# Layer 2's mixture of experts by lists: where the list is made, how deep the ring of gathered rows is, and when the output rows are fetched and summed

## The chip, the cores and the metric

The kernel runs on one core of one Trainium2 chip. The metric is the device time of one execution in microseconds. Three runs of the kernel before took 878.51, 871.72 and 876.23 us, median 876.23.

The core's engines work from queues of their own and wait for each other by semaphores: TensorE (PE in the profile; its weight loads are PEld), VectorE (DVE), ScalarE (ACT), GpSimd (POOL) and SyncE (SP), which issues most of the transfers.

## The reference

The input x is 8 sequences of 128 tokens of 128 numbers, f32. Four layers follow, each of an attention, a cross attention and a feed-forward part, and after each part `x = layernorm(x + part(x))`. The change lies in the feed-forward part of layer 2 and touches what stands next to it. That part is itself a small block: an attention, then eight experts of which each token uses two.

```python
        x = x + ao @ wo                                     # attention of the block
        h = _rmsnorm(x, ln2_w)
        probs = jax.nn.softmax(h @ router_w, axis=-1)
        topv, topi = jax.lax.top_k(probs, TOPK)             # 2 of 8
        topv = topv / jnp.sum(topv, axis=-1, keepdims=True)
        weights = jnp.sum(jax.nn.one_hot(topi, E) * topv[..., None], axis=-2)
        gate = jnp.einsum('bsd,edm->bsem', h, w_gate)       # d = 128, m = 448
        up = jnp.einsum('bsd,edm->bsem', h, w_up)
        act = jax.nn.silu(gate) * up * weights[..., None]
        moe = jnp.einsum('bsem,emd->bsd', act, w_down)
        return x + moe
```

After it come the layer norm and the first part of layer 3, a recurrence over the tokens of each sequence (a scan).

## The kernel before

The kernel doesn't compute all eight experts for every token. Class `ListedExperts` makes lists. The 1024 tokens are taken in two halves of 512. Each half has 1024 pairs of a token and one of its two experts; the pairs are sorted by expert and padded, each expert's to whole items of 128 rows, which gives at most 15 items a half (`N8`), 30 in all. The steps, by their methods:

- `rows` stores the half's normed tokens in DRAM. `route` makes the router's probabilities and ranks.
- `places(i)` counts, by products with ones (`ps_place` on PE) and small operations of DVE, which slot each pair has: its item `it` and its row `s` in it. From these come two sets of one-hot matrices, `s16` (tile `e_s`, on DVE) and `r16` (tile `e_r`, which holds the token's number in two digits: the partition, and j of 0 to 3). Before the change POOL makes `r16`: one operation for the first digit (L1004), six for the second (L1007) and two fills (L1009). `places` ends with each item's expert and with `place`, each pair's row in the output.
- `lists(i)` multiplies the two (`ps_ids`, PE), turns the digits into token numbers (`e_low` on ACT, `e_ids` on DVE), and issues 15 indirect gathers from the POOL queue (`e_xg`, L1030), one for each item's 128 rows of 512 bytes. All 30 share a ring of eight buffers, so that a gather waits for the transposition eight items earlier.
- `loaded(k)` has SP load item k's expert weights (704 KB) into one of five buffers; `turned(k)` transposes its rows (`ps_T` on PE, L1060; ACT copies them to `e_xT`, L1065); `up(k)` makes gate and up (`ps_g`, `ps_u` on PE; Silu to `e_g` on ACT, L1075; their product `e_h` on DVE, L1077); `down(k)` makes `ps_o` on PE, ACT copies it to `e_y` (L1087) and SP stores it to DRAM as `l_out` (L1088).
- `run` goes through the items k. Its order for PE is: transposition of k+1, gate and up of k, down of k-1, and then the extra steps given for k. The second half's `route`, `places` and `lists` are such steps, at k = 2, 6 and 8; the first half's sums are one at k = 17.
- `sums(i)` issues eight indirect gathers (`e_y`, L1114) that fetch each token's two output rows from DRAM, and adds them, weighted, to the block's x in eight DVE operations (`fin_h`, L1122). `f.norm` then makes the layer norm: statistics (L345, L346), a square root on ACT (`sd`, L335, which needs a table load), `rstd` (L337), four `x_nat` (L351). `f.turn` transposes the result (`ps_T`, L329; `x_T`, L409).

Around the items, `idle(n)` issues n products of 128x512 whose result isn't used; they keep PE busy. Layer 3's first part begins with a projection of each half (`ps_proj`), a gate and a product (`l_g`, ACT; `l_u`, DVE) and scans (`l_st`, DVE).

What sets the order: in this stage PE's instructions stand in the order of the source (`tc.manual_schedule` for PE). The other engines' orders are made by the scheduler when the kernel is built; their queues are then run strictly in that order. So a DVE operation that waits holds back all that stand behind it.

Of the kernel before, what the change touches and what calls it, by code (L numbers as in the profile page):

```python
# [10 lines left out]
BF16 = mybir.dt.bfloat16  # L11
# [4 lines left out]
ALU = mybir.AluOpType  # L16
# [4 lines left out]
P = 128  # L21
B = 8
T = 128
D = 128
# [117 lines left out]
N8 = (2 * 4 * T + E2 * (T - 1)) // T  # L142
# [16 lines left out]
def tile_decoder(  # L159
# [21 lines left out]
    nc = tc.nc  # L181
# [3 lines left out]
    work = ctx.enter_context(tc.tile_pool(name="work", bufs=3))  # L185
# [51 lines left out]
    def cst(name):  # L237
        a, b = CONST[name]
        return const_sb[:, a:b]
# [56 lines left out]
    def mm(dst, lhsT, rhs, start=True, stop=True):  # L296
        nc.tensor.matmul(dst, lhsT, rhs, start=start, stop=stop)  # L297
# [7 lines left out]
    def spread(ap, n):  # L305

        return ap.unsqueeze(2).to_broadcast([ap.shape[0], ap.shape[1], n])

    def repeat(ap, n):

        return ap.unsqueeze(1).to_broadcast([ap.shape[0], n, ap.shape[1]])

    def idle(n, rhs=None):

        ps = ps_sc.tile([P, 512], F32, tag="sc", name="ps_idle")
        for _ in range(n):
            mm(ps, begin_bf, repeat(begin_bf if rhs is None else rhs, 4))
# [597 lines left out]
    class ListedExperts:  # L915
# [52 lines left out]
        def places(self, i):  # L968

            used = self.used[i]  # L970
            ps = ps_out.tile([P, 5, 8], F32, tag="out", name="ps_place")
            for j in range(4):
                mm(ps[:, j], below_bf, used[:, j], True, j == 0)
                for k in range(j):
                    mm(ps[:, j], begin_bf, used[:, k], False, k == j - 1)
            for j in range(4):
                mm(ps[:, 4], begin_bf, used[:, j], j == 0, j == 3)
            tidx = cst("tidx")
            more = self.few("more", [P, 8, 4])
# [12 lines left out]
            nc.vector.tensor_reduce(slot, own.rearrange("p k j e -> p (k j) e"), AX.X, ALU.add)  # L992
            above = self.few("above", [P, 8, N8 - 1])
            nc.vector.scalar_tensor_tensor(
                above, repeat(tidx[:, 1:N8], 8), float(T), spread(slot, N8 - 1), ALU.mult, ALU.is_le
            )
            nc.vector.tensor_reduce(it, above, AX.X, ALU.add)
            nc.vector.scalar_tensor_tensor(s, it, -float(T), slot, ALU.mult, ALU.add)
            self.s16 = work.tile([P, 8, P], BF16, tag="g_gt", name="e_s16", bufs=1)
            nc.vector.tensor_tensor(self.s16, spread(s, P), repeat(tidx, 8), ALU.is_equal)  # L1000
            item = self.few("item", [P, 8, N8])
            nc.vector.tensor_tensor(item, spread(it, N8), repeat(tidx[:, 0:N8], 8), ALU.is_equal)
            self.r16 = self.few("r16", [P, 8, 2, N8], BF16)
            nc.gpsimd.tensor_scalar(self.r16[:, :, 0, :], item, cst("index"), None, ALU.mult)  # L1004
            for j in range(1, 4):
                for k in range(2):
                    nc.gpsimd.tensor_scalar(self.r16[:, 4 * k + j, 1, :], item[:, 4 * k + j, :], float(j), None, ALU.mult)  # L1007
            for k in range(2):
                nc.gpsimd.memset(self.r16[:, 4 * k, 1, :], 0.0)  # L1009
            past = self.few("past", [1, N8, 8])  # L1010
            nc.vector.tensor_tensor(past, spread(tidx[0:1, 0:N8], 8), repeat(ends[0:1], N8), ALU.is_ge)
            of = self.few("of", [1, N8])
            nc.vector.tensor_reduce(of, past, AX.X, ALU.add)
            self.experts[i] = self.few("exp", [1, N8], I32, 2)
            nc.vector.tensor_scalar_min(self.experts[i], of, 7.0)
            self.place[i] = self.few("place", [P, 8], U32, 2)
            nc.vector.tensor_copy(self.place[i], slot)

        def lists(self, i):

            ps = ps_out.tile([P, 2, N8], F32, tag="out", name="ps_ids")
            for k in range(8):
                mm(ps, self.s16[:, k, :], self.r16[:, k], k == 0, k == 7)
            self.ids[i] = self.few("ids", [P, N8], U32, 2)
            low = self.few("low", [P, N8])
            nc.scalar.copy(low, ps[:, 1])
            nc.vector.scalar_tensor_tensor(self.ids[i], ps[:, 0], 4.0, low, ALU.mult, ALU.add)
            for o in range(N8):
                self.xg[N8 * i + o] = xg = self.few("xg", [P, D], bufs=8)
                nc.gpsimd.indirect_dma_start(  # L1030
                    out=xg, out_offset=None, in_=self.rows_d[i],
                    in_offset=bass.IndirectOffsetOnAxis(ap=self.ids[i][:, o : o + 1], axis=0),
                )
# [53 lines left out]
            nc.scalar.copy(y, po)  # L1087
            nc.sync.dma_start(out=self.out_d[i][T * o : T * (o + 1), :], in_=y)  # L1088

        def run(self, pool, amid):  # L1090
            self.items = pool
            n = 2 * N8
            for k in range(4):
                self.loaded(k)
            self.turned(0)
            for k in range(n + 1):
                if k + 4 < n:
                    self.loaded(k + 4)
                if k + 1 < n:
                    self.turned(k + 1)  # L1100
                if k < n:
                    self.up(k)
                if k > 0:
                    self.down(k - 1)
                for step in amid.get(k, ()):
                    step()

        def sums(self, i, more):

            ys = []  # L1110
            for k in range(2):
                for j in range(4):
                    y = self.late(f"y{k}", [P, D], bufs=4)
                    nc.gpsimd.indirect_dma_start(  # L1114
                        out=y, out_offset=None, in_=self.out_d[i],
                        in_offset=bass.IndirectOffsetOnAxis(ap=self.place[i][:, 4 * k + j : 4 * k + j + 1], axis=0),
                    )
                    ys.append(y)
            h = work.tile([P, 4, D], F32, tag="fin_h", name="fin_h", bufs=2)
            for k in range(2):  # L1120
                for j in range(4):
                    nc.vector.scalar_tensor_tensor(  # L1122
                        h[:, j, :], ys[4 * k + j], self.w[i][:, k, j : j + 1], h[:, j, :] if k else more[:, j, :],
                        ALU.mult, ALU.add,
                    )
            return h
# [604 lines left out]
    def second_layers(f1, decay):  # L1731
        with tc.tile_pool(name="l2x", bufs=1, side="right") as keep:
# [3 lines left out]
            with tc.manual_schedule(engines={mybir.EngineType.PE}):  # L1736
# [38 lines left out]
                m = ListedExperts(w_moe2, msc("rw2"), 0.0, vec("ln2"), "l2")  # L1775
# [6 lines left out]
                f2 = Later()  # L1782
# [424 lines left out]
    f2 = second_layers(l1_ffn(x, xT), decay)  # L2207
# [174 lines left out]
```

## Time and profile before

| | us |
|---|---|
| runs, lowest, median, highest | 871.72, 876.23, 878.51 |
| the profiled execution's own time | 879.0 |
| its span | 877.2 |
| busy in it: PE, DVE, ACT, POOL | 727.6, 545.1, 418.1, 177.2 |
| first list: first ps_ids, first gather, first transposition | 582.61, 585.08, 588.13 |
| second list: first gather, thirteenth | 625.41, 650.20 |
| first half's output gathers, first and last issue | 651.44, 661.43 |
| last down product, its copy | 692.8 to 693.5, 693.60 |
| last half's output gathers done, last sum | 708.2 |

Times in the trace are counted from the span's start. A timeline row gives start, duration, engine, line, what is written from what, the number of instructions in the row and, in brackets, how long the engine stood idle before it and what released it; "issue" is idle time for which the profile shows no wait, "remote" a release by something that it can't name. A row of windows gives a stretch, then busy time of the engines in it, the clock granted to PE as a share of full speed, and the busy share of the DMA engines. A row of waits gives who waited for whom: total, number of times, longest. PE's ends are modelled by the profiler, and its records are pipelined, so neighbouring rows overlap a little.

### The profile page before, as it was taken

How to read it: one execution, taken by the hardware profiler on the slowest of the kernel's cores; microseconds unless marked ns; L12 is line 12 of the kernel's file. 1: busy time of each engine (PE TensorE's matmuls, PEld its weight loads, DVE VectorE, ACT ScalarE, POOL GpSimd, SP SyncE). 2: the span in 40 equal slices, each digit the busy share in tenths (PEclk: the TensorE clock that was granted, in tenths of full speed). 3: DMA queues.
4: the chain of work that ended last, by engine and by line, in shares of the span. 5: the costliest groups of instructions: out<-in, count | busy, mean ns of one | idle time of the engine just before them, and what ended most of it. 6: DMA issues, size and time to landing. Idle time of an engine off the chain costs nothing. (4 is left out here: it accounts for less than half of the span.)

```text
span 877.2 us, 14577 instructions
## 1 busy us (share of the span) xinstructions
PE 727.6 (83%) x4790; PEld 501.6 (57%) x4790; DVE 545.1 (62%) x1561; ACT 418.1 (48%) x963; POOL 177.2 (20%) x373
## 2 busy tenths in 40 slices
PE   8879999999988687439888879769997959888883
PEld 4758776665655454115345445449997726655552
DVE  4677786685476665898777766653424166656663
ACT  2234355333566663453186555625334422566662
POOL 1210100010011300001120203044442130056660
PEclk8689999999999799759999999987997978999997
DMA  9310000000000000000000000055896365011111
GB/s 358 121 37 1 1 1 1 1 0 1 1 1 1 1 1 1 1 0 1 0 1 1 1 1 1 13 190 142 263 328 198 97 277 217 1 34 37 33 35 40
DMA packets 22771, 53.57 MB, mean 61 GB/s; under 512 B 3904, under 2 KB 14144, under 8 KB 21280
## 3 DMA queue, kind: packets, MB, share of 16 engines
q1 hardware_dynamic: 20640, 47.55, 16.0%
q0 software_dynamic: 1472, 3.02, 1.5%
q10 hardware_dynamic: 576, 2.00, 0.6%
q8 instruction: 39, 0.64, 0.3%
q14 instruction: 44, 0.36, 0.1%
HBM read 46.39 MB, written 3.01 MB: 56 GB/s over the span
## 5 line engine op out<-in xcount | busy, mean ns | idle before, releaser
L534 DVE TENSOR_REDUCE at_mx<-ps_s 128x8 f32<-128x1024 f32 x48 | 56.9, 1216 | 42.2 <-PE ps_s L297 42.2
L537 ACT ACTIVATE at_s<-ps_s,at_mx 128x128 f32<-128x128 f32 x192 | 53.7, 390 | 38.1 <-DVE at_mx L534 38.1
L297 PEld LDWEIGHTS ps_o<-w_moe,e_h 128*128 128x128 f32 (+1 forms) x496 | 62.7, 198 | 12.6 <-issue 10.7
L297 PE MATMUL ps_o<-w_moe,e_h 128*128 128x128 f32 (+1 forms) x496 | 66.0, 283 | 4.7 <-issue 3.8
L546 ACT ACTIVATE at_pT<-ps_T 128x512 f32<-128x512 f32 x96 | 53.6, 601 | 33.4 <-PE ps_T L329 33.3
L297 PE MATMUL ps_idle<-begin_bf 128*128 128x512 bf16 x226 | 63.2, 419 | 4.0 <-DVE l_s L658 2.9
L329 PE MATMUL ps_T<-const_sb,at_s 128*128 128x128 f32 x384 | 60.5, 295 | 7.2 <-ACT at_s L537 5.1
L2119 POOL COPY l_wg<-w 128x64 f32 x192 | 49.2, 302 | 81.5 <-ACT l_wd L2115 53.3
L297 PEld LDWEIGHTS <-begin_bf 128*128 128x128 bf16 x273 | 28.0, 111 | 62.5 <-issue 41.2
L329 PEld LDWEIGHTS ps_T<-const_sb,at_s 128*128 128x128 f32 x384 | 46.2, 146 | 28.8 <-issue 10.7
L1077 DVE TENSOR_TENSOR e_h<-e_g,ps_u 112x512 f32<-112x512 f32 x30 | 20.6, 688 | 57.8 <-PE ps_u L297 32.2
L297 PEld LDWEIGHTS ps_acc<-l_wd,l_h 128*128 128x128 f32 x256 | 31.0, 191 | 38.4 <-ACT l_h L2141 38.4
L297 PE MATMUL ps_acc<-l_wd,l_h 128*128 128x128 f32 x256 | 37.1, 288 | 13.2 <-ACT l_h L2141 13.2
L805 ACT ACTIVATE x_p<-ps_s,x_mx 128x256 f32<-128x256 f32 x64 | 30.0, 474 | 33.9 <-DVE x_mx L801 26.3
L517 POOL TENSOR_TENSOR kx<-xa_k,const_sb 128x512 f32<-128x512 f32 x16 | 16.8, 1052 | 130.2 <-PE ps_s L297 74.1
L2115 ACT COPY l_wd<-w 64x128 f32 x96 | 28.4, 296 | 26.1 <-PE ps_acc L297 17.5
L297 PE MATMUL ps_s<-kvT,x_q 128*128 128x256 f32 x128 | 35.3, 402 | 4.0 <-ACT x_p L805 4.0
L297 PE MATMUL ps_av<-at_pT,vaug 128*32 128x128 f32 x768 | 31.1, 284 | 9.0 <-ACT at_pT L546 8.5
L335 ACT ACTIVATE sd<-ln_mv,eps 128x4 f32<-128x4 f32 x28 | 8.3, 297 | 62.7 <-DVE ln_mv L346 54.8
L894 DVE TENSOR_TENSOR e_h<-e_g,ps_u 128x512 f32<-128x512 f32 x32 | 21.8, 684 | 24.1 <-PE ps_u L297 20.8
L297 PE MATMUL ps_u<-e_xT,w_moe 128*112 128x128 f32 x240 | 34.4, 288 | 1.1 <-issue 1.1
L297 PE MATMUL ps_g<-e_xT,w_moe 128*112 128x128 f32 x240 | 34.5, 291 | 1.0 <-ACT e_xT L1065 1.0
(481 smaller groups left out, 1705.5 us busy)
## 6 DMA issues: line engine op xcount, KB each, us to landing
w_moe<-in_w_moe_dram SPq DMA_DIRECT2D x30, 704.0 KB
w<-in_w_moe_dram SPq DMA_DIRECT2D x10, 1024.0 KB
w_moe<-in_w_moe_dram SPq DMA_DIRECT2D x4, 768.0 KB
l_wd<-w SPq DMA_DIRECT2D x96, 32.0 KB
l_out<-e_y SPq DMA_DIRECT2D x30, 64.0 KB
sq_sb<-in_squares_dram SPq DMA_DIRECT2D x1, 1152.0 KB
row_sb<-in_rows_dram ACTq DMA_DIRECT2D x1, 784.0 KB
const_sb<-in_consts_dram ACTq DMA_DIRECT2D x1, 630.5 KB
```

Source lines behind the costliest of these rows:

```text
L297: nc.tensor.matmul(dst, lhsT, rhs, start=start, stop=stop)
L329: nc.tensor.transpose(ps[:, i, :], src[:, i, :], ident)
L335: nc.scalar.activation(sd, var, AF.Sqrt, bias=eps)
L517: nc.gpsimd.tensor_tensor(kx, repeat(job.k(b), 4), spread(cst(job.hm), T), ALU.mult)
L534: nc.vector.tensor_reduce(nmx[k], flat, AX.X, ALU.max, negate=True)
L537: nc.scalar.activation(sh[u][1][:, i // 4, i % 4, :], flat[:, i, :], AF.Identity, bias=nmx[1][:, i : i + 1])
L546: to_T(sh[u][g // 2][:, g % 2], lambda t: nc.scalar.activation(p, t, AF.Exp))
L805: nc.scalar.activation(pr[:, j, :], ps[:, j, :], AF.Exp, bias=mx[:, j : j + 1], accum_out=sm[:, j : j + 1])
L894: nc.vector.tensor_tensor(h[:, c, :], g, pu, ALU.mult)
L1077: nc.vector.tensor_tensor(self.h[k], g, pu[:C2], ALU.mult)
L2115: nc.scalar.copy(dst, src)
L2119: nc.gpsimd.tensor_copy(dst, src)
```

## The change

In five parts.

1. `r16` is made by two DVE operations, before `s16`, instead of by nine of POOL.
2. The second half's gathered rows have a ring of their own of 15 buffers (`e_xg1`); the first half's keep the ring of eight.
3. `run` becomes `step(k)`. The gathers of the output rows become a method of their own, `fetched(i)`, issued at k = 15 for the first half and after the loop for the second; the sums follow at k = 21 (before: both at k = 17). Both go through the four rows j of a token with its two experts inside; before, all first experts came before all second ones.
4. The second half's `places` and `lists` come one item earlier, at k = 5 and 7.
5. The idle products: 16 instead of 10 after the first list, 30 instead of 14 at the end, there ahead of the last sums. The first half's transpositions `f.turn(0)` move from the end to k = 29, between the last two down products.

```diff
-            self.s16 = work.tile([P, 8, P], BF16, tag="g_gt", name="e_s16", bufs=1)
-            nc.vector.tensor_tensor(self.s16, spread(s, P), repeat(tidx, 8), ALU.is_equal)
             item = self.few("item", [P, 8, N8])
             nc.vector.tensor_tensor(item, spread(it, N8), repeat(tidx[:, 0:N8], 8), ALU.is_equal)
             self.r16 = self.few("r16", [P, 8, 2, N8], BF16)
-            nc.gpsimd.tensor_scalar(self.r16[:, :, 0, :], item, cst("index"), None, ALU.mult)
-            for j in range(1, 4):
-                for k in range(2):
-                    nc.gpsimd.tensor_scalar(self.r16[:, 4 * k + j, 1, :], item[:, 4 * k + j, :], float(j), None, ALU.mult)
-            for k in range(2):
-                nc.gpsimd.memset(self.r16[:, 4 * k, 1, :], 0.0)
+            nc.vector.tensor_scalar(self.r16[:, :, 0, :], item, cst("index"), None, ALU.mult)
+            nc.vector.tensor_tensor(
+                self.r16[:, :, 1, :].rearrange("p (k j) o -> p k j o", j=4),
+                item.rearrange("p (k j) o -> p k j o", j=4),
+                tidx[:, 0:4].unsqueeze(1).unsqueeze(3).to_broadcast([P, 2, 4, N8]), ALU.mult,
+            )
+            self.s16 = work.tile([P, 8, P], BF16, tag="g_gt", name="e_s16", bufs=1)
+            nc.vector.tensor_tensor(self.s16, spread(s, P), repeat(tidx, 8), ALU.is_equal)
...
             for o in range(N8):
-                self.xg[N8 * i + o] = xg = self.few("xg", [P, D], bufs=8)
+                self.xg[N8 * i + o] = xg = (self.late if i else self.few)(
+                    f"xg{i}", [P, D], bufs=N8 if i else 8
+                )
...
+        def fetched(self, i):
+
+            self.ys = {}
+            for j in range(4):
+                for k in range(2):
+                    self.ys[k, j] = y = self.late(f"y{k}", [P, D], bufs=4)
                     nc.gpsimd.indirect_dma_start(
                         out=y, out_offset=None, in_=self.out_d[i],
                         in_offset=bass.IndirectOffsetOnAxis(ap=self.place[i][:, 4 * k + j : 4 * k + j + 1], axis=0),
                     )
-                    ys.append(y)
+
+        def sums(self, i, more):
+
             h = work.tile([P, 4, D], F32, tag="fin_h", name="fin_h", bufs=2)
-            for k in range(2):
-                for j in range(4):
+            for j in range(4):
+                for k in range(2):
                     nc.vector.scalar_tensor_tensor(
-                        h[:, j, :], ys[4 * k + j], self.w[i][:, k, j : j + 1], h[:, j, :] if k else more[:, j, :],
+                        h[:, j, :], self.ys[k, j], self.w[i][:, k, j : j + 1], h[:, j, :] if k else more[:, j, :],
                         ALU.mult, ALU.add,
                     )
             return h
...
                 m.lists(0)
-                idle(10)
+                idle(16)
+            pe = mybir.EngineType.PE
+            with tc.manual_schedule(engines={pe}):
                 m.weights_of(0)
                 f = Finish(None)
                 with tc.tile_pool(name="l2m", bufs=1) as pool:
-                    m.run(pool, {
+                    m.items = pool
+                    amid = {
                         1: (lambda: f2.done(1, last, 1),),
                         2: (lambda: m.route(1, f2.h2T),),
-                        6: (lambda: m.places(1),),
-                        8: (lambda: m.lists(1),),
+                        5: (lambda: m.places(1),),
+                        7: (lambda: m.lists(1),),
                         9: (lambda: m.weights_of(1),),
-                        N8 + 2: (lambda: f.norm(0, m.sums(0, f2.xx[:, 0:4, :])),),
-                    })
+                        N8: (lambda: m.fetched(0),),
+                        N8 + 6: (lambda: f.norm(0, m.sums(0, f2.xx[:, 0:4, :])),),
+                        2 * N8 - 1: (lambda: f.turn(0),),
+                    }
+                    for k in range(2 * N8 + 1):
+                        m.step(k)
+                        for step in amid.get(k, ()):
+                            step()
+                    m.fetched(1)
+                    idle(30)
                     f.norm(1, m.sums(1, f2.xx[:, 4:8, :]))
                 epool.__exit__(None, None, None)
-                idle(14)
-                f.turn(0)
             return f
```

`step(k)` holds what the loop of `run` held for item k, in the same order.

More of the change, by code (lines that the diff above doesn't have):

```diff
@@ L1088, in down, with step @@
             nc.sync.dma_start(out=self.out_d[i][T * o : T * (o + 1), :], in_=y)
-        def run(self, pool, amid):
-            self.items = pool
+        def step(self, k):
             n = 2 * N8
[L1093 to L1110, printed above, removed]
-            for k in range(2):
-                for j in range(4):
-                    y = self.late(f"y{k}", [P, D], bufs=4)
+            if k == 0:
+                for o in range(4):
+                    self.loaded(o)
+                self.turned(0)
+            if k + 4 < n:
+                self.loaded(k + 4)
+            if k + 1 < n:
+                self.turned(k + 1)
+            if k < n:
+                self.up(k)
+            if 0 < k <= n:
+                self.down(k - 1)
+        def fetched(self, i):
[3 more added lines that the diff above has]
+                    self.ys[k, j] = y = self.late(f"y{k}", [P, D], bufs=4)
                     nc.gpsimd.indirect_dma_start(
@@ L1117, in sums @@
                     )
-                    ys.append(y)
+        def sums(self, i, more):
             h = work.tile([P, 4, D], F32, tag="fin_h", name="fin_h", bufs=2)
-            for k in range(2):
-                for j in range(4):
+            for j in range(4):
+                for k in range(2):
                     nc.vector.scalar_tensor_tensor(
-                        h[:, j, :], ys[4 * k + j], self.w[i][:, k, j : j + 1], h[:, j, :] if k else more[:, j, :],
+                        h[:, j, :], self.ys[k, j], self.w[i][:, k, j : j + 1], h[:, j, :] if k else more[:, j, :],
                         ALU.mult, ALU.add,
```

## The prediction

> **What bounds the kernel now.** I first read the table of windows through the expert stage, to see where TensorE stops being busy.
>
> ```profile
> 620.00:630.00 10.00, 9.72 (x93) 9.50 (x92) 4.17 (x10) 3.65 (x10) 6.52 (x11) 1.00 0.87 249
> 630.00:640.00 10.00, 10.00 (x91) 9.77 (x90) 2.75 (x4) 3.88 (x12) 4.72 (x6) 1.00 0.90 265
> 640.00:650.00 10.00, 10.00 (x94) 10.00 (x93) 2.75 (x4) 3.98 (x11) 2.95 (x4) 1.00 1.00 380
> 650.00:660.00 10.00, 7.41 (x66) 7.04 (x64) 2.03 (x5) 2.12 (x6) 7.54 (x8) 1.00 0.76 244
> 660.00:670.00 10.00, 7.39 (x32) 6.91 (x33) 5.33 (x19) 4.86 (x9) 3.34 (x4) 0.51 0.49 121
> ```
>
> The columns are PE, PEld, DVE, ACT and POOL busy, then granted clock, DMA share and GB/s. From 630 to 650 PE is full: the stage is bound by it, at 2.75 us an item (ps_o of items 16 and 17 start at 648.76 and 651.51). From 650 to 670 it is neither full nor, later, at full clock. The timelines of PE, DVE, ACT and POOL there say why.
>
> ```profile
> 654.26 1.06 PE L297 MATMUL ps_o<-w_moe,e_h 112*128 112x128 f32 x8
> 660.98 2.08 PE L297 MATMUL ps_o<-w_moe,e_h 112*128 112x128 f32 x8 [3.34 <-issue]
> 668.61 1.90 PE L297 MATMUL ps_o<-w_moe,e_h 112*128 112x128 f32 x8
> 672.20 1.06 PE L297 MATMUL ps_o<-w_moe,e_h 112*128 112x128 f32 x8
> ```
> ```profile
> 651.78 0.69 DVE L1077 TENSOR_TENSOR e_h<-e_g,ps_u 112x512 f32<-112x512 f32 x1 [2.06 <-PE ps_g L297]
> 654.55 0.35 DVE L1122 SCALAR_TENSOR_TENSOR fin_h<-e_y,e_w,l_xx 128x128 f32<-128x128 f32 x1 [2.09 <-DMA e_y<-l_out,e_place]
> 658.87 0.65 DVE L1122 SCALAR_TENSOR_TENSOR fin_h<-e_y,e_w,l_xx 128x128 f32<-128x128 f32 x2 [0.75 <-issue]
> 660.24 0.69 DVE L1077 TENSOR_TENSOR e_h<-e_g,ps_u 112x512 f32<-112x512 f32 x1 [0.72 <-remote]
> ```
> ```profile
> 655.90 0.60 ACT L1075 ACTIVATE e_g<-ps_g 112x512 f32<-112x512 f32 x1 [2.39 <-PE ps_T L1060]
> 664.47 0.27 ACT L1087 COPY e_y<-ps_o 128x128 f32<-128x128 f32 x1 [7.97 <-PE ps_T L1060]
> ```
> ```profile
> 651.44 0.94 POOL L1114 DMA_INDIRECT e_y<-l_out,e_place  x1 [0.30 <-issue]
> ```
>
> The down products of items 18, 19, 20 and 21 start at 654.26, 660.98, 668.61 and 672.20: 17.94 us for three items that take 8.25, a loss of 9.7 us. Two things hold them up.
>
> First, the sums. Four sums of the first half stand in DVE's queue ahead of item 19's e_h; the gathers that feed them start at 651.44, and the fourth sum ends at 659.52.
>
> Second, less plain: e_h of item 19 runs not at 659.52 but at 660.24, and ACT copies item 18's ps_o at 664.47, although PE's record has that product finished at 655.32 (654.26 + 1.06). What waits for PE is released up to 9.1 us late. The same shows under an earlier row of gathers, issued 1.25 us apart from 625.41 to 630.47:
>
> ```profile
> 628.34 1.04 PE L297 MATMUL ps_u<-e_xT,w_moe 128*112 128x128 f32 x8
> 629.21 1.06 PE L297 MATMUL ps_o<-w_moe,e_h 112*128 112x128 f32 x8
> ```
> ```profile
> 631.17 0.69 DVE L1077 TENSOR_TENSOR e_h<-e_g,ps_u 112x512 f32<-112x512 f32 x1 [3.75 <-PE ps_T L1060]
> ```
> ```profile
> 632.58 0.27 ACT L1087 COPY e_y<-ps_o 128x128 f32<-128x128 f32 x1 [3.03 <-PE ps_u L297]
> ```
>
> There ps_u ends at 629.38 and is used at 631.17 (1.8 us late), and ps_o ends at 630.27 and is used at 632.58 (2.3 late). A third place is the stage's start, under gathers in close order from 585 to 599: ps_u of item 1 ends at 596.60 and its e_h runs at 600.89. From 634.5 to 650 the gathers stand 2.75 us apart, because the ring of eight makes each wait for a transposition, and nothing is late (ps_o ends 649.82, its copy starts 649.85). So **late release goes with gathers in close order**. That it is caused by them is my inference.
>
> **The change, part by part** (differences in us; minus is faster).
>
> *Sums and output gathers.* The DVE order of the built kernel does not put the sums six items later: five of them still stand between e_h of items 18 and 19, three between 19 and 20. What changes is the supply. The second half's input gathers are out of the way, so the first output gather waits only for the landing of item 14's store (issued 644.77, landing marks about 648.1) and can start at 648.4, not 651.44; the eighth is issued at 657.1, not 661.43. The fifth is issued at 653.4 and lands 2.2 to 4.2 later (the range of 656.43 to 658.62 and of 652.69 to 656.87), so item 19's e_h, due at 654.5 (651.78 + 2.75), is free of sums at 656.5 to 658, half covered by the 2.06 us that DVE idles per item. Close gathers end 4.3 us earlier, hence also the late releases. Bounds: 0 (as late as now) and -9.7. I take **-4.5**, near the 4.3. On ACT the sd and its table load (1.28 + 0.30) now come ahead of item 19's e_y; both stood ahead of item 22's e_xT before, so nothing further waits.
>
> *Ring of fifteen.* It removes this wait of POOL:
>
> ```profile
> POOL e_xg L1030 <- PE ps_T L1060: 19.4, 9, 3.7
> ```
>
> That wait cost PE nothing, since PE was full. What goes with it is the spacing: fifteen gathers now run at 1.25 us from 623.4 to about 642, beside full PE and a DMA share of 0.87 to 1.00. Ten more than now are in close order. Lower row: the five at 625 to 631 cost PE 0.30 (ps_T of three items at 630.10, 632.90, 635.90: 5.80 for 5.50), 0.06 each, so +0.6. Upper row: the ten from 650 to 662 stand beside a loss of 9.7, 0.97 each, so +9.7. By the end of the five the lateness was 2.3, already over DVE's 2.06 of slack; ten more gathers span 4.5 items, and 0.24 to 2.2 beyond slack in each (2.3 to the start's 4.3) is 1 to 10. I take **+3.5**. A rule speaks against this term: the Trainium skill, "SBUF — State Buffer" (opening part on the two sides), holds that transfers and engines use separate ports and cannot slow each other; by it the term would be 0 and the total 3.5 lower. The late releases at 631 and 664 do not fit that rule, though no run here yet isolates them.
>
> *List on DVE.* Two e_r operations go ahead of at_o (579.69), which leads through at_oT, ps_o and ps_ids to the first gather. Nearest row: e_item, 128x120, 0.28 at 578.37, issued 0.19 apart. Two cost 0.4 to 0.6: **+0.4**. POOL's e_r ended at 581.62, before ps_ids (582.61), so nothing is won there. In the second list PE's 0.27 wait for POOL's e_r (at 624.32) goes: **-0.3**; DVE has slack for the rest. The step one item earlier only moves work.
>
> *Sixteen idle products for ten.* Ten took 3.37 (582.87 to 586.24), then PE stood 1.89 until the first ps_T at 588.13. Six more take 2.0, so 0.1 late, or 2.6 at half clock (0.43 each), 0.7 late. If the clock (0.74 in 590 to 600) stays up for one more stretch, the 3.82 of ps_g and ps_u at 590.49 becomes 2.1; but item 0's e_g waits for ACT's table load until 593.93 anyway. Bounds -3.4 and +0.7; I take **-0.7**.
>
> *End of the stage.* Four transpositions (0.60 at 696.38) now precede the last down product: +0.6. The thirty idle products take 6.84 (14 took 3.19) and end about 701; ps_proj (1.93) then ends at 703, before the last sum at 708.21, so they are hidden. In DVE's queue l_u (0.65, at 706.07 between gathers before) moves behind the aggregates with the scans (1.39) and still ahead of rstd: +0.65; the new order of sums leaves fewer statistics behind the last one: about -0.05 to -0.5. I take **+1.2** in all, bounds +0.5 and +2.
>
> *Sum*: -4.5 + 3.5 + 0.4 - 0.3 - 0.7 + 1.2 = -0.4. The profiled execution took 879.0 (span 877.2), so it would take 878.6; on the median of the runs, 876.2 (871.7 to 878.5), 875.8, say **876**.
>
> A second rule may be set beside the gathers' landing: "DMA: Bandwidth & Descriptors", section on the anatomy of a SWDGE transfer, gives 2.0 us plus bytes/436e3, an estimated 2.15 for 64 KB; by it alone the fifth gather would land at 655.6 and the sums would hold nothing. The 4.2 measured at 652.69 under load says it can be twice that.
>
> **Rivals.**
>
> *Close gathers cost as much everywhere as at 650 to 662* (slower). Place: items 13 to 18 under the fifteen, then 18 to 20 under the eight. Price: +9.7 for ten more, and only -1.9 at the sums (two gathers fewer at 0.97), with the rest +0.6: +8.4, 884.6; a half-clock stretch of 3.4 us more makes 888. It decides once e_h or e_y follow PE's end by more than some 3 us for several items. For it: 4.3 and 9.1 us late at two of three places. Against: 0.30 lost at the third, which is the place in question.
>
> *Late release goes with the sums, not the gathers* (faster). Then the fifteen cost 0, the stall shrinks by 8.7, the start gives 2: -8.7 + 0.4 - 0.3 - 2 + 1.2 = -9.4, 866.8. For it: 650 to 670 is the only place with a large loss, and the sums are there. Against: ACT's copy at 664.47 waits for no sum.
>
> *The change does not do what it says.* DVE still meets the sums at item 19; if the output gathers land as late as now, -1 + 0.6 + 0.6 = +0.2, 876.4.
>
> **How the numbers follow.** Forecast 0.40, slower rival 0.28, faster rival 0.18, no effect 0.14. What differs by under 1% (8.8 us) can hardly be told from no change here. Faster 0.18, same 0.54, slower 0.28. The range reaches from below the faster rival, 865, to the slower one at half clock, 889.
>
> **What would show it.** Right: POOL's fifteen gathers 1.25 us apart, then DVE's e_h 3 to 4 us after PE's ps_u in several of items 11 to 17, ps_T more than 2.75 apart there; output gathers starting some 3 us sooner after item 14's store; items 18 to 21 in about 13 us, not 17.9. Wrong: PE busy 10.00 in every window under the fifteen gathers (ring term 0), items 18 to 21 again in 18 us, or ps_proj after the last sum.

## The result, and the profile after

The changed kernel takes 888.73 us (median of six runs, 887.42 to 892.05); the kernel before 876.84 (871.72 to 878.67, six runs). The medians lie 11.9 us apart, 1.4%. The record's ratio of the runs, which is not the ratio of the medians, is 1.0169, with an interval of 1.0146 to 1.0193. By either the change makes the kernel slower. The profiled execution took 890.67 with a span of 888.8, against 879.0 and 877.2 before, so its span is 11.6 us longer.

First the table of windows of the changed kernel, through the same part of the expert stage and with the same columns as before (PE, PEld, DVE, ACT and POOL busy, granted clock, DMA share, GB/s).

```profile
620.00:630.00 10.00, 8.72 (x78) 8.28 (x76) 1.66 (x4) 2.34 (x7) 7.14 (x8) 1.00 0.82 229
630.00:640.00 10.00, 4.46 (x14) 3.44 (x15) 0.00 (x0) 1.13 (x3) 7.01 (x8) 0.55 0.47 129
640.00:650.00 10.00, 7.99 (x44) 7.50 (x44) 2.06 (x3) 2.73 (x8) 0.00 (x0) 0.59 0.59 165
650.00:660.00 10.00, 10.00 (x94) 10.00 (x93) 2.59 (x4) 3.99 (x10) 0.00 (x0) 1.00 0.90 272
660.00:670.00 10.00, 9.99 (x91) 9.79 (x89) 2.87 (x8) 2.80 (x8) 5.73 (x6) 1.00 0.90 289
670.00:680.00 10.00, 5.83 (x36) 5.80 (x37) 5.06 (x18) 5.35 (x10) 3.14 (x3) 0.83 0.63 193
```

The loss is in one place. In 630 to 640, where PE was full before, it now runs 14 products in ten microseconds instead of 91, and DVE runs nothing at all. POOL's 7.01 are the second half's gathers: the fifteen stand 1.25 us apart from 620.73 to 638.20. From 650 to 660, with no gather on POOL, PE is full again. The next hole, 670 to 680, follows the eight output gathers (662.57 to 671.38).

PE's timeline in the first hole:

```profile
628.62 1.16 PE L297 MATMUL ps_o<-w_moe,e_h 112*128 112x128 f32 x8 [1.17 <-issue]
...
631.25 2.05 PE L297 MATMUL ps_g<-e_xT,w_moe 128*112 128x128 f32 x8 [1.36 <-issue]
633.46 0.37 PE L297 MATMUL ps_u<-e_xT,w_moe 128*112 128x128 f32 x1 [0.16 <-issue]
634.86 0.37 PE L297 MATMUL ps_u<-e_xT,w_moe 128*112 128x128 f32 x1 [1.03 <-issue]
636.26 0.37 PE L297 MATMUL ps_u<-e_xT,w_moe 128*112 128x128 f32 x1 [1.02 <-issue]
...
642.76 2.08 PE L297 MATMUL ps_o<-w_moe,e_h 112*128 112x128 f32 x8 [0.53 <-DVE e_h L1079]
...
648.20 1.06 PE L297 MATMUL ps_o<-w_moe,e_h 112*128 112x128 f32 x8
```

Eight products of one ps_u, which take 1.04 us in an undisturbed item, are strung out over nine, and the idle time before them is "issue": they wait for nothing that the profile shows. The down products of items 9, 10 and 11 start at 628.62, 642.76 and 648.20, 19.58 us for two items that take 5.50. ACT and DVE, in their timelines:

```profile
639.09 0.60 ACT L1077 ACTIVATE e_g<-ps_g 112x512 f32<-112x512 f32 x1 [7.90 <-remote]
```
```profile
642.01 0.69 DVE L1079 TENSOR_TENSOR e_h<-e_g,ps_u 112x512 f32<-112x512 f32 x1 [13.45 <-remote]
```

The table of waits from 620 to 645 puts it in sums (who waited for whom: total, times, longest):

```profile
DVE e_h L1079 <- remote: 13.5, 1, 13.5
...
ACT e_g L1077 <- remote: 7.9, 1, 7.9
PEld ps_u L297 <- issue: 6.5, 6, 1.6
PE ps_u L297 <- issue: 5.8, 8, 1.0
```

None of these names a transfer or another engine's work; the table's other rows of ACT and DVE name PE. ACT's e_g needs ps_g, whose last product ends at 633.30 by PE's record; it runs at 639.09, 5.8 us late. This is the late release of the prediction, now as a whole item's stall. It ends about 4 us after the last close gather is issued (638.20 to 642.0).

The other places that the prediction named. The output gathers start at

```profile
662.57 0.94 POOL L1113 DMA_INDIRECT e_y<-l_out,e_place  x1 [23.43 <-DMA l_out<-e_y]
```

held by item 14's store, as worked out: 6.1 us after the start of that item's down product, where it was 8.2 before and 5.1 had been worked out. The end of the stage, in DVE's timeline:

```profile
718.07 0.35 DVE L1123 SCALAR_TENSOR_TENSOR fin_h<-e_y,e_w,fin_h 128x128 f32<-128x128 f32 x1 [0.86 <-DMA e_y<-l_out,e_place]
...
718.88 0.66 DVE L1860 TENSOR_TENSOR l_u<-l_g,ps_proj 64x512 f32<-64x512 f32 x1
719.58 1.36 DVE L1862 TENSOR_TENSOR_SCAN l_st<-l_A,l_u 64x128 f32<-64x128 f32 x4
720.87 0.14 DVE L337 RECIPROCAL rstd<-sd 128x4 f32<-128x4 f32 x1
721.04 1.12 DVE L351 TENSOR_SCALAR x_nat<-fin_h,ln_mv,rstd 128x128 f32<-128x128 f32 x4
```

Here l_u does stand behind the last sum, and ps_proj (done at 712.55) doesn't hold it. The same points in both traces give the account (start of the down product ps_o of an item):

| from, to | before | after | difference |
|---|---|---|---|
| span's start to e_rank, the stage's first list | 574.03 | 572.26 | -1.8 |
| e_rank to ps_o of item 0 | 22.40 | 22.24 | -0.2 |
| items 0 to 8 | 30.03 | 30.04 | 0.0 |
| items 8 to 12 | 11.29 | 26.41 | +15.1 |
| items 12 to 18 | 16.51 | 16.50 | 0.0 |
| items 18 to 21 | 17.94 | 14.58 | -3.4 |
| items 21 to 28 | 19.15 | 19.15 | 0.0 |
| item 28 to x_nat | 19.37 | 19.86 | +0.5 |
| x_nat to the span's end | 166.5 | 167.8 | +1.3 |

Before rounding they add to 11.6. Against 2.75 us an item, items 9 to 11 lose 15.4 us here; the expectations below count 14.4. The first row lies ahead of the change. In the last, the second half's ps_proj takes 3.27 instead of 2.49, +0.8.

### The profile page after: what moved, and what is told of

Read it like the earlier page. It is cut to its first block, busy times and chain, and to the rows that moved or that the text cites. A ratio compares the mean times of both kernels' runs of the same rounds, so it can differ in the third digit from the quotient of the medians.

```text
span 888.8 us, 14604 instructions
## 1 busy us (share of the span) xinstructions
PE 734.5 (83%) x4812; PEld 504.0 (57%) x4812; DVE 546.5 (61%) x1565; ACT 417.8 (47%) x963; POOL 172.3 (19%) x355
## 5 line engine op out<-in xcount | busy, mean ns | idle before, releaser
L297 PE MATMUL ps_idle<-begin_bf 128*128 128x512 bf16 x248 | 67.0, 412 | 3.2 <-DVE l_s L658 2.1
L297 PEld LDWEIGHTS <-begin_bf 128*128 128x128 bf16 x295 | 29.9, 109 | 64.5 <-issue 41.0
L297 PE MATMUL ps_u<-e_xT,w_moe 128*112 128x128 f32 x240 | 37.0, 293 | 8.0 <-issue 7.9
L297 PEld LDWEIGHTS ps_u<-e_xT,w_moe 128*112 128x112 f32 x240 | 32.6, 195 | 9.2 <-issue 9.2
```

## The experiments

r_after and r_after2 are the changed kernel unaltered. The runs came on four chips, each group with the kernel before on the same one. The ratios are the record's, to that kernel (they differ a little from those of the medians); the kernel before took 868.86 us on chip A, 876.63 on B, 874.42 on C and 875.52 on D. "At 2.75" means that the down products of the items stand 2.75 us apart, which is PE full.

| kernel, chip | us | ratio, interval | down product to down product |
|---|---|---|---|
| e1_shared8, A | 870.27 | 1.0013, 0.9991 to 1.0036 | 9 to 18 at 2.75; 19, 20: 7.25, 4.52 |
| e2_ring15_only, A | 875.99 | 1.0076, 1.0050 to 1.0102 | 13: 6.68; 19, 20: 8.94, 4.74 |
| e3_paced15, A | 869.57 | 1.0006, 0.9988 to 1.0025 | 9 to 18 at 2.75; 19, 20: 7.84, 4.50 |
| e4_paced_all, A | 865.04 | 0.9955, 0.9938 to 0.9973 | 9 to 27 at 2.75 |
| r_after, B | 892.41 | 1.0168, 1.0114 to 1.0222 | 9, 10, 11: 5.61, 13.51, 4.86; 19, 20: 7.47, 4.50 |
| e5_no_weights, B | 892.37 | 1.0168, 1.0123 to 1.0212 | 10, 11: 15.61, 5.32; 18, 19, 20: 7.76, 5.49, 3.12 |
| e6_plain_rows, B | 876.12 | 0.9986, 0.9966 to 1.0006 | 9 to 18 at 2.75; 19, 20: 7.43, 5.49 |
| e7_late_sums, B | 894.29 | 1.0197, 1.0147 to 1.0248 | 9, 10, 11: 5.60, 13.61, 4.82; 19, 20: 7.46, 4.49 |
| r_after2, C | 890.17 | 1.0191, 1.0145 to 1.0237 | 9, 10, 11: 4.14, 14.71, 4.62; 19, 20: 7.40, 4.35 |
| e2b_ring15_only, C | 888.58 | 1.0169, 1.0124 to 1.0215 | 11, 12: 15.49, 5.49; 19, 20: 7.27, 4.51 |
| e3b_paced15, C | 877.09 | 1.0023, 0.9999 to 1.0047 | 9 to 18 at 2.75; 19, 20, 21: 6.35, 7.91, 3.73 |
| e8_best, C | 868.02 | 0.9931, 0.9901 to 0.9961 | 11 to 21 at 2.75; 22, 23: 5.31, 4.52 |
| e9_best2, D | 866.48 | 0.9897, 0.9873 to 0.9921 | 9, 10, 13: 4.35, 3.08, 3.22; 15 to 27 at 2.75 |
| e10_in_order, D | 889.42 | 1.0149, 1.0114 to 1.0184 | 9, 10, 11: 4.17, 14.62, 5.13; 19, 20: 7.66, 4.48 |
| e11_threes, D | 876.48 | 1.0018, 0.9997 to 1.0039 | 9 to 17 at 2.75; 18, 19, 20: 4.55, 9.12, 3.89 |
| e12_two_an_item, D | 878.45 | 1.0035, 1.0010 to 1.0061 | 13, 14: 2.92, 3.79; 18, 19, 20: 4.34, 8.90, 5.46 |

### Which part of the change: the ring

e1 is the changed kernel with the ring of eight for both halves; e2 and e2b are the kernel before with the ring of fifteen as its only change. The edit of e1 (e2's is the reverse of it, in the kernel before):

```diff
-                self.xg[N8 * i + o] = xg = (self.late if i else self.few)(
-                    f"xg{i}", [P, D], bufs=N8 if i else 8
-                )
+                self.xg[N8 * i + o] = xg = self.few("xg", [P, D], bufs=8)
```

> The changed kernel with one part undone: the second half's gathered rows share the ring of eight again. Theory A (close gathers): fifteen gathers 1.25 us apart slow PE itself. Then at most some five run in close order, the 14.4 us lost between the down products of items 8 and 11 fall below 1, and the time falls from 888.7 to 873 to 877. Rival B (another part of the change, such as the list made on DVE or the second list one item earlier, causes the stall): 886 to 890 as now.

> The kernel before with one part of the change alone: a ring of fifteen of its own for the second half's gathered rows. Theory A: the stall of some 14 us appears here too, 886 to 892 against 876.8 before. Rival B: 875 to 878, as before.

On chip A the ring alone costs 7.1 us, and without it the rest of the change is worth nothing that can be measured (+1.4, its interval holding 1). But chip A shows the cost in another form. In e2's timeline of PE:

```profile
633.82 1.93 PE L297 MATMUL ps_g<-e_xT,w_moe 128*112 128x128 f32 x8 [2.09 <-DMA w_moe<-in_w_moe_dram]
```

PE waits for an expert's weights, item 13 comes 3.9 us late, and no release is late under the close gathers. Where the rest of the 7.1 us lies isn't shown, since the kernel before has no trace on chip A. Items 1 and 2 of this chip's kernels come 3.2 and 3.6 us after their forerunners, where they come 5.2 and 6.7 in the profile before. So A couldn't test the mechanism, and the same kernel was run again on C beside the unaltered change.

> The changed kernel, unaltered, to stand beside the next three on one chip. Two kinds of chip have shown so far: on one (kernel before 876 to 877) the changed kernel takes 888 to 892 and PE is released late under close gathers; on the other (kernel before 868.9) nothing was late behind PE. Where the kernel before takes 876 here, 888 to 893; where it takes 869, theory A gives no PE stall and 871 to 876 by late weights alone.

> The kernel before with the ring of fifteen alone, a second time, to stand beside the changed kernel on one chip. Where the kernel before takes 876: theory A gives a stall of 12 to 15 us under the fifteen gathers, 887 to 892, which would put the whole loss down to this one part. Where it takes 869: 875 to 877, as the first time. If on a chip of the first kind it stays under 880, the loss needs another part of the change as well.

There the ring alone costs 14.2 us (888.58 - 874.42), all but 1.6 of the change's 15.8. The row of windows of e2b is that of the changed kernel, and so is PE's timeline, single products of ps_u 0.7 to 2.1 us apart:

```profile
630.00:640.00 10.00, 3.47 (x15) 2.77 (x16) 0.00 (x0) 1.13 (x3) 7.56 (x9) 0.63 0.49 134
```

### What about the ring: the close order, or the depth

e3 and e3b keep the ring of fifteen and all else of the change, but each of the second half's gathers is put one item later than the one before, by a copy of POOL that needs the item's e_y.

```diff
+            if after is not None:
+                nc.gpsimd.tensor_copy(xg[:, 0:1], after[:, 0:1])
             nc.gpsimd.indirect_dma_start(
...
+                    for o in range(N8):
+                        amid[7 + o] = amid.get(7 + o, ()) + (lambda o=o: m.gathered(1, o, m.last_y),)
```

> The changed kernel with its ring of fifteen, but the second half's gathers issued one an item: ahead of each, POOL copies one column of the item's e_y into the gather's buffer, so it waits for that item. Theory A: with 2.75 us between gathers the 14.4 us at items 9 to 11 are gone though the ring is fifteen, 873 to 877. Rival C (the ring's place or size in memory causes the stall, not the spacing): 886 to 890. The eight output gathers still come in close order, so the 6.3 us lost at items 19 and 20 stay in both.

> The changed kernel with its ring of fifteen and the second half's gathers paced one an item, a second time. Where the kernel before takes 876: theory A gives items 9 to 18 at 2.75 us and 874 to 878; a ring of fifteen that stalls whatever the spacing gives 888 or more. Where it takes 869: 869 to 871 as the first time.

On C the loss under the input rows is gone, and the row of windows is full:

```profile
630.00:640.00 10.00, 10.00 (x94) 10.00 (x93) 2.75 (x4) 3.95 (x10) 4.45 (x7) 1.00 0.99 309
```

Same ring, same gathers, same other changes: what costs is that they come close. What is left of the change against before is then +2.7 (interval -0.1 to +4.1). Two finer doses on D say how close is too close: e11 issues them in groups of three, a group every third item, and e12 two an item.

```diff
-                        amid[7 + o] = amid.get(7 + o, ()) + (lambda o=o: m.gathered(1, o, m.last_y),)
+                        amid[7 + o // 3 * 3] = amid.get(7 + o // 3 * 3, ()) + (lambda o=o: m.gathered(1, o, m.last_y),)
```

(e12: `7 + o // 2`.)

> The changed kernel with its ring of fifteen and the second half's gathers in groups of three in close order, one group every three items. The first five close gathers of the kernel before cost 0.30 us, and release was late from the fourth on. Theory A with a backlog that builds up over a row: under 1 us lost at items 9 to 18, 875 to 879 where the kernel before takes 874 to 877. If any two close gathers beside PE's products are enough, 5 us or more are lost.

> The changed kernel with its ring of fifteen and two gathers an item, 1.38 us apart on average instead of 1.25. If what counts is the rate (a backlog that grows as long as gathers come faster than they are worked off, with PE's lateness from the fourth on), the stall at items 9 to 12 stays at 8 us or more, 884 to 890. If a pause in each item is enough to clear it, under 2 us are lost, 875 to 879.

Groups of three cost nothing at items 9 to 17. Two an item would be 1.38 us a gather on the mean, hardly more than the 1.25 of the close row. In e12's trace, though, the gathers come in fours, 1.28 to 1.42 us apart, with 2.1 to 2.8 us between the fours: 1.60 on the mean. They cost 1.2 us (2.92 and 3.79 at items 13 and 14), not 15: ACT's copies run 1 to 3 us late again and again, and catch up. So a steady rate of 1.38 wasn't tried; what is shown is that fours with such a pause cost little. In both the output gathers then come close behind and cost 9 to 11 us at items 18 to 20.

### What in the close gathers: the weights beside them, the addresses, or the form

e5 leaves out the 704 KB loads from item 5 on (the items reuse the five buffers' weights). e6 replaces the second half's fifteen indirect gathers by plain loads of the same size from the same queue, all of the first 128 rows. e10 keeps the indirect form and has all fifteen fetch rows 0 to 127 in order. Their edits, in this order:

```diff
+            if k >= 5:
+                self.wt[k] = self.five[k % 5]
+                return
...
+                if i:
+                    nc.gpsimd.tensor_copy(xg[:, 0:1], low[:, o : o + 1])
+                    nc.gpsimd.dma_start(out=xg, in_=self.rows_d[i][0:T, :])
+                    continue
...
-            nc.vector.scalar_tensor_tensor(self.ids[i], ps[:, 0], 4.0, low, ALU.mult, ALU.add)
+            if i:
+                nc.vector.scalar_tensor_tensor(
+                    self.ids[i], ps[:, 0], 0.0, cst("index").to_broadcast([P, N8]), ALU.mult, ALU.add
+                )
```

> The changed kernel again, unaltered, on the chip of this set: the four experiments before ran on a chip where the kernel before takes 868.9, and showed no late release behind PE at all, while the ring of fifteen alone cost 7 us there by a wait for an expert's weights. Theory A (close gathers slow PE) then holds only for the chip of the first comparison, and the loss here is 4 to 9 us with a wait for w_moe in the chain; if A holds on every chip, PE's products stand 0.7 us apart under the fifteen gathers and the loss is 10 to 14.

> The changed kernel without the weight loads of items 5 to 29: those items use the weights that lie in the five buffers, which leaves out 25 of the 30 experts' matrices that belong to them and 704 KB an item. Theory D (the fifteen gathers and the weight loads share the DMA engines, and the weights come late): the stall under the fifteen gathers is gone, items 9 to 18 run at 2.75 us, and the stores land sooner. Theory A (the gathers slow PE by themselves): the stall at items 9 to 13 stays.

> The changed kernel with the fifteen indirect gathers of the second half replaced by fifteen plain loads of 128 rows from the same queue, each behind a POOL copy that waits for the second list; which leaves out the selection of the rows. If the indirect form matters (descriptors made by POOL row by row), the stall under the fifteen is gone. If any close row of POOL's transfers does it, or their 64 KB each beside the weights, it stays, at 4 to 9 us where the weights come late and over 10 where PE is slowed.

> The changed kernel with its fifteen close indirect gathers, but each fetches rows 0 to 127 of the second half in order, still behind the second list; which leaves out the selection of the rows by expert. If the scatter of the addresses slows PE, the stall under the fifteen is gone and the time is near the kernel before, as with plain loads. If the indirect form does it (POOL writes one descriptor a row), the stall of 13 to 15 us at items 9 to 11 stays where the kernel before takes 874 to 877.

The same row of windows for e5, e6 and e10, in this order:

```profile
630.00:640.00 10.00, 4.26 (x15) 3.38 (x15) 0.00 (x0) 0.94 (x3) 7.48 (x8) 0.57 0.27 59
```
```profile
630.00:640.00 10.00, 10.00 (x93) 10.00 (x92) 2.75 (x4) 3.98 (x12) 1.58 (x3) 1.00 1.00 347
```
```profile
630.00:640.00 10.00, 3.04 (x11) 2.53 (x11) 0.00 (x0) 0.53 (x2) 6.57 (x7) 0.51 0.43 131
```

With the DMA engines at 0.27 and 59 GB/s, PE stalls as before: it isn't a fight for transfers with the weights. With plain loads the DMA engines are at 1.00, the rows come still faster from the same queue, and PE is full:

```profile
622.21 4.88 POOL L1034 DMA_DIRECT2D e_xg<-l_rows  x9
```

Nine in 4.88 us, against one in 1.25. The shorter row isn't the reason: all fifteen plain loads take 8.9 us (622.21 to 631.10), as long as a row of eight close gathers (8.8 us), which costs 6.5 at items 18 to 21 of r_after. And indirect gathers of rows in order stall PE just as lists do. So neither the amount moved, nor the queue, nor the scatter of the rows does it; it is the indirect form, issued in a long close row. What in that form does it, no run separates.

### The sums

In e7 the order of DVE is that of the source from item 10 on, so that the first half's sums do stand behind e_h of item 21.

```diff
+                    with tc.manual_schedule(engines={pe, mybir.EngineType.DVE}):
+                        for k in range(10, 2 * N8 + 1):
```

> The changed kernel with DVE's order from item 10 on kept as written, so that the first half's eight sums stand in DVE's queue behind e_h of item 21, six items after their gathers, as the source says. If the sums' wait holds back items 19 and 20, the 6.3 us lost there (down products 18 to 21) fall below 1.5, and the time is 4 to 6 less than the changed kernel in this set. If the late releases behind PE hold them, or sd and its table load on ACT, 3 us or more stay lost.

Items 18 to 21 take 14.71 us in e7 and 14.72 in r_after on the same chip. The sums ahead of item 19 can be taken away and nothing is gained there: with no sum ahead of it, that item's e_h waits for PE.

```profile
672.45 0.69 DVE L1079 TENSOR_TENSOR e_h<-e_g,ps_u 112x512 f32<-112x512 f32 x1 [8.00 <-PE ps_u L297]
```

So the row of eight close output gathers is enough to hold these items on chip B. e7's profile is 2.5 us longer than r_after's and has two further slow items, 22 and 23 (5.25 and 4.43), where the sums and the layer norm now stand.

On chip A, where nothing is late behind PE, the sums are enough by themselves. In e3 there, item 19's e_h runs right behind a sum that waited for its gather's landing, and PE waits for it:

```profile
654.00 0.35 DVE L1131 SCALAR_TENSOR_TENSOR fin_h<-e_y,e_w,l_xx 128x128 f32<-128x128 f32 x1 [0.42 <-DMA e_y<-l_out,e_place]
...
654.36 0.65 DVE L1086 TENSOR_TENSOR e_h<-e_g,ps_u 112x512 f32<-112x512 f32 x1
```
```profile
655.07 1.88 PE L297 MATMUL ps_o<-w_moe,e_h 112*128 112x128 f32 x8 [4.92 <-DVE e_h L1086]
```

### Kernels that pace every gather

e4 is e3 with the output gathers, too, one an item (items 17 to 24), the sums three items behind each in a DVE order kept as written from item 10 on, and the first half's norm at item 28. e8 also gives the first half a ring of four instead of eight and moves the norm of the first half to the last items. e9 is e8 with the output gathers moved to items 20 to 27, after the input gathers, the second half's first three input gathers at once, and the norm, 20 idle products and the transpositions at the end. The gathers and sums of e9:

```diff
+                    for o in range(N8):
+                        at = 7 if o < 3 else 5 + o
+                        amid[at] = amid.get(at, ()) + (lambda o=o: m.gathered(1, o, m.last_y),)
+                    for o in range(8):
+                        at = N8 + 5 + o
+                        amid[at] = amid.get(at, ()) + (lambda o=o: m.fetch_one(0, o, m.last_y),)
+                        at = N8 + 8 + o
+                        amid[at] = (lambda o=o: m.sum_one(0, o, f2.xx[:, 0:4, :]),) + amid.get(at, ())
```

> As the one before, and the first half's eight output gathers too are issued one an item (items 17 to 24, each behind a POOL copy of one column), each of the eight sums three items after its gather, with DVE's order from item 10 on kept as written, so that no sum stands ahead of an e_h that is due. Theory A: no row of close gathers is left beside the items after the first list, so items 3 to 28 run at 2.75 us throughout: 14.4 and 6.3 us less than the changed kernel, some 866 to 870. If late releases come from gathers at any spacing, or from the transfers of the weights, a stall stays in items 9 to 24 and the time is over 873.

> All gathers that run beside items spaced: the first half's ring is four deep instead of eight, the second half's gathers and the first half's output gathers are paced one an item, the eight sums come three items after their gathers with DVE's order kept from item 10 on, the layer norm of the first half comes after e_h of item 29, and its transpositions between twelve and eighteen idle products at the end. Theory A, where the kernel before takes 876: the late releases at items 1 and 2 shrink too, items 3 to 29 run at 2.75 us, 858 to 864. Where it takes 869: 861 to 865. If pacing itself costs (a gather late for its transposition), PE waits for e_xg appear and the time is over 868.

> The best version, spaced further: in the kernel with all gathers paced, input and output gathers still fell in pairs in items 17 to 21, six in close order at 651 to 658, and items 22 and 23 lost 4.4 us. Here the second half's first three gathers come at once and the rest one an item, done by item 19; the output gathers come one an item in items 20 to 27, the sums three items later, the first half's layer norm and transpositions behind the last product. Theory A, where the kernel before takes 874 to 877: no item after the third over 3.2 us, 862 to 866. Where it takes 869: 861 to 865. If what held items 22 and 23 was not the close gathers, they still lose 4 us.

In e4, on A, the items 9 to 27 stand at 2.75 throughout, also 19 and 20, 4.5 us less than e3. That isn't the spacing: e4's input and output gathers fall together, eleven of them 1.3 to 1.7 us apart from 642.71 to 656.62, and PE stays full. What e4 takes away on this chip is the sums' wait. In e8, on C, the stage's start shows the effect of spacing: with a ring of four for the first half item 1 comes after 3.19 us, where the ring of eight takes 5.23 (r_after2), 5.18 (e2b) and 5.42 (e3b); item 2, at 3.60, isn't clearly better (3.70, 6.69 and 3.70). e8 put an input and an output gather into the same items, six of them close at 651 to 658, and paid 5.31 and 4.52 at items 22 and 23; e_g there runs after 3.67 us of "remote". e9 mends that, 9.0 us below the kernel before on the same chip (6.9 to 11.1), a gain of all its moves together. PE is full through both of the former holes:

```profile
640.00:650.00 10.00, 10.00 (x94) 10.00 (x93) 2.75 (x4) 3.93 (x11) 4.01 (x8) 1.00 1.00 351
650.00:660.00 10.00, 10.00 (x93) 10.00 (x92) 2.56 (x4) 3.99 (x10) 4.45 (x7) 1.00 1.00 279
```

It still loses 1.9 us at items 9 and 10, where its group of three follows close on the first half's last gathers, and 0.5 at item 13, where ps_g waits for weights.

## Why the prediction was wrong

It forecast 876 and no change; the kernel became 12 us slower. The range, up to 889, holds the time because of the slower rival, and that rival is what happened: close gathers cost as much, and more, at items 9 to 12 as at 650 to 662. Its own price was off as well: +9.7 for the ring and -1.9 at the sums, where +15.1 and -3.4 were measured. That its 888 with a half-clock stretch comes so near is luck. Step by step:

- *Late release goes with gathers in close order*, an inference there, is shown by e3b against r_after2 (same kernel, gathers spaced, stall gone) and narrowed to indirect gathers by e6 and e10. The faster rival, that it goes with the sums, falls with e7 and e2b.
- **The failed step is the size of "Ring of fifteen"**: +3.5 was taken, +15.1 measured in the profile, and 14.2 for the ring alone. The choice went to the nearer row, five close gathers that cost 0.30 in all. Both ends had been made linear in the number of gathers, 0.06 and 0.97 each, and the upper one, 9.7, was too low as well. The cost isn't so much a gather: three close cost 0 (e11), five 0.3 (before), eight 6.25 to 6.5 (items 18 to 21 of the changed kernel in its three profiles, over their 8.25) and fifteen 15.1. From eight to fifteen that is about 1.25 us each, the spacing itself: once the first few are through, PE all but stands for as long as the row lasts. The two rows of the trace before lay on both sides of a step, and a straight line through either was the error. The row itself gave the sign: its lateness had grown from 1.8 to 2.3 us by its fifth and last gather.
- *What goes with the removed wait is the spacing*: right, and the heart of it. The wait of 19.4 us on POOL cost nothing and kept the gathers 2.75 us apart.
- *Sums and output gathers*: -4.5 taken, -3.4 measured at items 18 to 21. The first gather waits for item 14's store, as worked out. But the two causes named there don't add: the close gathers hold these items without the sums (14.71 us in e7), and the sums without late release (14.51 in e1, on chip A). That the gain comes from eight close gathers in place of ten (before, two input gathers stood ahead of and among them, at 650.20 and 657.68) fits the rows, but no run shows it by itself.
- *List on DVE*: +0.4 taken; e_rank to at_o grows from 5.66 to 6.04, 0.38. *Sixteen idle products and the second list*: the clock in 590 to 600 does stay higher, 0.83 for 0.74, and from e_rank to item 8 the kernel gains 0.15 us (52.28 for 52.43). With the 0.38 of the list that leaves -0.5 where -1.0 had been taken, all of it ahead of item 0.
- *End of the stage*: +1.2 taken; +0.5 up to x_nat, with the idle products and ps_proj hidden as said, and +1.3 behind it, of which 0.8 lie in the second ps_proj, which had not been named.

The rule that was set against the ring's term, the Trainium skill's "SBUF — State Buffer" (its opening part, and "Who interferes with whom": a DMA never contends with a compute engine), would have put the term at 0. For plain loads this case agrees: e6 has the DMA engines at 1.00 and PE at 10.00. For long rows of indirect gathers it doesn't: PE at 4.26 of 10 us beside a DMA share of 0.27 in e5. The measurement decides. Whether the port that the page speaks of has a part in it, no run here shows.

Two things stay open. What in the chip slows PE: the profile calls the wait "issue", and names nothing. And why chip A, the fastest, shows none of it: there the ring cost 7 us, 3.9 of them at an item with late weights, and why the weights are late there was not tried.

## What to carry to other kernels

A wait that costs nothing may be what spaces the transfers behind it: before a ring is deepened, look at how close its transfers will then come and what runs beside them. Beside a full TensorE, on three of the four chips here, indirect gathers had to be paced, one an item or three with a pause between, by a shallow ring or by a dependency. Pacing the second half's gathers alone took the loss from 15.8 us to 2.7 (e3b); with the other gathers paced and the sums and the norm moved the kernel gains 9 (e9). And where a queue's order is made by a scheduler, "six items later" in the source says little. Which of two neighbours holds an engine is told only by moving each of them, and either may be enough alone.

## What the runs showed of the hardware

- Under a long row of close indirect gathers PE falls to about one instruction, weight load or product, in 0.70 us: in the changed kernel products start at 633.46, 634.86 and 636.26 and the weight loads between them at 634.17 and 635.56, with 0.37 and 0.26 us of work in each. In r_after it also stands still for 5.60 us, up to 638.07, again by "issue". The weight loads' rows, from its timeline of PEld:

```profile
634.17 0.26 PEld L297 LDWEIGHTS ps_u<-e_xT,w_moe 128*112 128x112 f32 x1 [0.98 <-issue]
635.56 0.26 PEld L297 LDWEIGHTS ps_u<-e_xT,w_moe 128*112 128x112 f32 x1 [1.13 <-issue]
```

- The stall starts some four to six gathers into the row, and ends about 4 us after the row's last issue, taken by the next e_h (638.20 to 642.01; in e5 638.66 to 642.63; in r_after 638.78 to 643.30).
- The recorded end of a product and the moment its result is used lie up to 5.8 us apart here with no other wait in between (9.1 in the kernel before). An engine's idle time "remote", right after a PE row that looks finished, is the sign of it.
- Chips differ in this: the same ring costs 14.2 us on chip C by PE's stall, and 7.1 on chip A, where PE isn't stalled by gathers, not even by e4's eleven in a row, and one item loses 3.9 to late weights.
